# The queries of seven token blocks from seven half-size products instead of four full ones, with their cosine product put elsewhere and two rooms for the rotation

## The chip, the cores and the metric

The kernel runs on one core of a Trainium2 chip, as one launch. The metric is the device time of a whole execution in microseconds (us); the time of a kernel is the median of its runs. The profile is one more execution, taken by the hardware profiler. All data are float32.

The engines by the profile's names: PE is the matrix engine (PEld its loading of weights), DVE the vector engine, ACT the scalar engine, POOL GpSimd, and SP the queue that issues most DMAs. PE writes its products to PSUM, from which DVE and ACT read them.

## The reference, cut to what matters

A graph layer is followed by attention and a mixture of experts, over 4096 tokens of 256 features:

```python
def layer(x, adj, ...):
    f = layernorm(x)
    x = x + concat([f, (adj @ (f @ neigh_W.T)) / (adj.sum(1) + 1)]) @ lin_W.T   # graph
    h = rmsnorm(layernorm(x), ln1_w)
    q, k, v = h @ wq.T, h @ wk.T, h @ wv.T                     # 4 heads of q, 2 of k and v, 64 wide
    q = q * cos + rotate_half(q) * sin                         # the same for k
    ...                                                        # causal attention, projection
    ...                                                        # router, 2 of 8 experts, their sum
```

`rotate_half` puts the negated second half of a head before its first half. The change is in how `h @ wq.T` and the rotation of q are computed.

## The kernel before, in words

The tokens are eight blocks of 512. The first stage is the graph layer. `aggregate(b)` makes the product of adjacency row block b with the features, over eight steps jb. A step takes one 512 x 512 block of the adjacency, 1 MB, which `load` brings with a lead of three steps into three buffers `a`. Each step already uses Strassen's scheme in Winograd's form: `halve` makes the sums and differences S1 to S4 of the adjacency block on DVE (lines 495 to 498), one step ahead of their use; `halve_x` made those of the features earlier (lines 467 to 470); and PE does seven products of halves, in two parts each, into four PSUM tiles (line 538). S1 and S2 of even steps lie in the room of the last block's queries, and those of odd steps in `more_sums`. At the end of a row block DVE puts the seven products together (lines 547 to 560, line 546 on ACT).

Into the steps of `aggregate(b)` other work is sewn in at fixed places, between the fourth and the fifth of the seven products of a step or at its end: the last linear map of the row block before (`linear`, line 199), and from `qkv(b - 1)` the queries, keys and values of that row block. There is no scheduler: each engine takes its instructions in the order in which the program writes them. For a block, `qkv` does this:

- step 1: `scales` (statistics) and `turn_tables` (the tables of cosines and sines are transposed),
- step 2: `norm` and `leave` (the normed rows go to DRAM); at its end `fetch` brings them back into a room called `z`, and `spread_tables` copies the tables to all partitions,
- step 3, end: `turn` transposes `z` on DVE into `qT[b]`, features on partitions and tokens along the row (line 621),
- step 4: `values_and_logits` (line 632), then `turned_heads((2,))`, which makes k,
- step 5: `turned_heads((0, 1))`, which makes the two halves of q.

`turned_heads` multiplies on PE, 512 tokens wide, two products for each of its parts (line 648), into a PSUM tile of pool `p_pj`, which has two. DVE multiplies the result by the cosines (line 655), straight from PSUM into its place; four ACT copies put the swapped and signed quarters into the room `rot` (line 657); POOL multiplies them by the sines and adds them (lines 661 and 662). `rot` has one room, so the copies of the next part wait for POOL's addition. The room `z` is the place of the next block's queries, for the seventh block a tile of its own, `last_z`. The eighth block goes another way, in the attention stage.

The stages after it are attention with routing and then the experts. They are not touched.

Of the kernel before, what the change touches and what calls it, by code (L numbers as in the profile page):

```python
# [9 lines left out]
F32 = mybir.dt.float32  # L10
I32 = mybir.dt.int32
SP = mybir.EngineType.SP
AF = mybir.ActivationFunctionType
# [4 lines left out]
P = 128  # L18
# [4 lines left out]
NH, NKV, HD = 4, 2, 64  # L23
# [8 lines left out]
Q = HD // 2  # L32
# [34 lines left out]
def fast_kernel(  # L67
# [24 lines left out]
    nc = tc.nc  # L92
# [27 lines left out]
    for e in range(NE):  # L120
# [6 lines left out]
    wqkv_sb = const.tile([P, 2, 512 + NE], F32, name="wqkv_sb")  # L127
# [14 lines left out]
    qT = [  # L142
        qT_all[:, b * 1024 : (b + 1) * 1024].rearrange("p (c i) -> p c i", c=2)
        for b in range(NB)
    ]
# [43 lines left out]
    def in_order(x):  # L189
        return x.rearrange("p (g c d) -> p c g d", g=4, c=2)  # L190
# [68 lines left out]
    with (  # L259
# [37 lines left out]
        tables = {}  # L297
# [50 lines left out]
        def bounds():  # L348

            ps = p_pj.tile([P, 512], F32, tag="pj", name="p_bounds")  # L350
            gram = ps[:, 0 : 3 * HD].rearrange("p (m i) -> p m i", m=3)
            for m in range(3):
                for c in range(2):
                    for j in range(2):
                        head = wqkv_sb[:, c, m * P + j * HD : m * P + (j + 1) * HD]
                        nc.tensor.matmul(
                            gram[j * HD : (j + 1) * HD, m, :], head, head,
                            start=(c == 0), stop=(c == 1), skip_group_check=True,
                        )
            squares = gx.tile([P, HD], F32, tag="rot", name="squares", bufs=1)  # L360
            for m in range(3):
                nc.scalar.activation(
                    squares, gram[:, m, :], AF.Square, accum_out=norms[:, m : m + 1]
                )
# [12 lines left out]
        def router_wo():  # L377
            transposed_wo = qT[5][:, :, 0:C]
            ps = p_pj.tile([P, 512], F32, tag="pj", name="p_wo")
            for j in range(2):  # L380
                for c in range(2):
                    nc.tensor.matmul(
                        ps[:, j * NE : (j + 1) * NE], transposed_wo[:, c, j * P : (j + 1) * P],
                        wqkv_sb[:, c, QK : QK + NE], start=(c == 0), stop=(c == 1),
                    )
            nc.scalar.copy(
                wo_sb[:, :, C:], ps[:, 0 : 2 * NE].rearrange("p (j e) -> p j e", j=2)
            )

        def negate_weights():  # L390
            for k in range(2):
                nc.scalar.activation(
                    wn_less[:, k, :], wn_sb[:, k, :], AF.Identity,
                    bias=wn_sb[:, k, C - 1 : C], scale=-1.0,
                )
            nc.gpsimd.memset(m_sb[:, 0, C : C + 1], 0.0)
            nc.gpsimd.tensor_copy(m_sb[:, 1, C : C + 1], ident[:, P - 1 : P])
# [21 lines left out]
        G11, G12, G21, G22, T1, T2, T4 = range(7)  # L419
        T3 = G12  # L420
        HC = C // 2
        g = [gw.tile([P, 7, 2, HC], F32, name=f"g{b}") for b in range(NB)]
# [145 lines left out]
            )  # L568

        turning = [tc.dram_tile([512, C], F32, name=f"turning{n}") for n in range(2)]  # L570
        last_z = gs.tile([P, 1024], F32, name="last_z")

        def qkv(b):

            made = {}

            def scales():
                stats(gx, b)
                var = mv[b][:, :, 1:2]
                power(both[b], var, *BOTH)  # L580
                power(rstd[b], var, 1.0, EPS_LN)

            def norm():

                made["h0"] = [
                    t.rearrange("p (t c) -> p t c", t=2)
                    for t in (kT[b], vv[b].rearrange("p t c -> p (t c)"))
                ]
                for t in range(TB):
                    nc.vector.tensor_scalar(  # L590
                        in_order(made["h0"][t // 2][:, t % 2, :]), in_groups(res[b][:, t, :]),
                        mv[b][:, t, 0:1], both[b][:, t], op0=ALU.subtract, op1=ALU.mult,
                    )
                made["ratio"] = ratio(gx, b)

            def leave():

                for n, h0 in enumerate(made.pop("h0")):
                    nc.sync.dma_start(
                        turning[b % 2][n * 2 * P : (n + 1) * 2 * P].rearrange(  # L600
                            "(t p) c -> p t c", p=P
                        ),
                        h0,
                    )

            def fetch():

                made["z"] = qT_all[:, (b + 1) * 1024 : (b + 2) * 1024] if b + 2 < NB else last_z
                squares = turning[b % 2].rearrange("(m i) (g e) -> g i m e", i=Q, g=4)
                for n in range(4):  # L610
                    nc.sync.dma_start(
                        made["z"][n * Q : (n + 1) * Q].rearrange("p (m e) -> p m e", e=2 * Q),
                        squares[n],
                    )

            def turn():

                made["hT"] = qT[b]
                z = made.pop("z").rearrange("p (m c d) -> p c m d", c=2, d=Q)
                for c in range(2):  # L620
                    nc.vector.transpose(
                        qT[b][:, c, :].rearrange("p (m i) -> p m i", i=Q), z[:, c]
                    )

            def values_and_logits():
                for h in range(2):
                    pj = p_tr.tile([P, 2, 2, P], F32, tag="tr", name=f"pv_{b}_{h}")
                    pj = pj.rearrange("p c t i -> p c (t i)")
                    for i in range(2):
                        at = (2 * h + i) * P  # L630
                        for c in range(2):
                            nc.tensor.matmul(  # L632
                                pj[:, i, 0 : NE + P], made["hT"][:, c, at : at + P],
                                wqkv_sb[:, c, QK:], start=(c == 0), stop=(c == 1),
                            )
                    nc.scalar.copy(vv[b][:, 2 * h : 2 * h + 2, :], pj[:, :, NE : NE + P])  # L636
                    for i in range(2):
                        t = 2 * h + i
                        nc.scalar.activation(
                            first_lg[b][:, t, :], pj[:, i, 0:NE], AF.Copy,  # L640
                            scale=made["ratio"][:, t],
                        )

            def turned_heads(ms):
                pjs = [p_pj.tile([P, 512], F32, tag="pj", name=f"pq_{b}_{m}") for m in ms]
                for m, pj in zip(ms, pjs):
                    for c in range(2):
                        nc.tensor.matmul(
                            pj, wqkv_sb[:, c, m * P : (m + 1) * P], made["hT"][:, c, :],
                            start=(c == 0), stop=(c == 1),  # L650
                        )
                for m, pj in zip(ms, pjs):
                    to = kT[b] if m == 2 else qT[b][:, m, :]
                    rot = gx.tile([P, 512], F32, tag="rot", name=f"rot_{b}_{m}", bufs=1)
                    nc.vector.tensor_mul(to, pj, tables[b][:, 0, :])  # L655
                    for n in range(4):
                        nc.scalar.activation(  # L657
                            rot[n * Q : (n + 1) * Q, :], pj[(n ^ 1) * Q : ((n ^ 1) + 1) * Q, :],
                            AF.Copy, scale=1.0 if n % 2 else -1.0,
                        )  # L660
                    nc.gpsimd.tensor_mul(rot, rot, tables[b][:, 1, :])  # L661
                    nc.gpsimd.tensor_add(to, to, rot)

            return [
                [scales, lambda: turn_tables(b)], [norm, leave], [],
                [values_and_logits, lambda: turned_heads((2,))], [lambda: turned_heads((0, 1))],
            ], {
                (2, "end"): [fetch], (2, "loaded"): [lambda: spread_tables(b)],
                (3, "end"): [turn],
            }  # L670
# [34 lines left out]
                steps[jb, "end"] = [lambda b=jb + 3: turned_x(b)]  # L705
        steps[0].insert(1, lambda: turned_x(2))
        steps[3].append(load_rest)
        for jb, f in ((5, scale_rest), (6, bounds), (6, turn_wo), (7, router_wo)):
            steps[jb].append(f)
        behind, at_end = [], []  # L710
        for b in range(NB):
# [15 lines left out]
    with (  # L727
# [76 lines left out]
        probs, sums, accs, ys, flats, chosen, squares, picks, narrows = ({} for _ in range(9))  # L804
# [2021 lines left out]
```

## Time and profile before

| what | value |
|---|---|
| median of 3 runs | 1512.95 us (1511.27 to 1515.51) |
| the profiled execution's own time | 1511.47 us |
| its span, first to last instruction | 1509.8 us |
| PE busy | 1496.9 us, 99% |
| DVE busy | 1083.9 us, 72% |
| ACT busy, POOL busy | 544.9 us, 568.9 us |
| line 648, products of q and k | 84 records of 592 ns |
| line 655, DVE product with the cosines | 21 of 0.69 us |
| line 657, ACT copies into `rot` | 84 of 589 ns |
| line 661, POOL product with the sines | 21, 1636 ns in the mean |

A float32 matmul leaves two records, each with its load of weights. The duration of a record includes the flow through the array, in which the next one already runs, so durations add up to more than the time that PE needs; the distance between two starts is what a record costs. A row "x8" of the timeline is eight records in a run.

### The profile page before, as it was taken

The page shows a single profiled execution, that of the slowest core. Times are in us where ns is not written, and L with a number is a line of the kernel's source. Part 1 is how long each engine was busy: PE and PEld are TensorE (multiplying, and loading weights), DVE is VectorE, ACT ScalarE, POOL GpSimd, SP SyncE. Part 2 cuts the span into 40 slices and gives each one's busy share as a digit, 9 for nine tenths or more (in the row PEclk, how much of TensorE's full clock was granted, in tenths as well). Part 3 has the DMA queues.
Part 4 walks back from the last instruction along what each step waited for, and adds up shares of the span by engine and source line. Part 5 has one row for each costly group of instructions (what it writes and reads, how often), then busy time and mean ns, then how long its engine had stood idle before and what let it go on. Part 6 is the DMA issues. An engine that isn't in the chain of part 4 may idle for free. (4 is left out here: it accounts for less than half of the span.)

```text
span 1509.8 us, 28585 instructions
## 1 busy us (share of the span) xinstructions
PE 1496.9 (99%) x10731; PEld 1102.8 (73%) x10731; DVE 1083.9 (72%) x2239; ACT 544.9 (36%) x975; POOL 568.9 (38%) x649
## 2 busy tenths in 40 slices
PE   9999999999999999999999999999999999999997
PEld 7888888888888544444444444358899999999996
DVE  7855666656765577779879879795676877777872
ACT  2102011021020455655665655653222334343341
POOL 2102122121221331374565553551523464554542
PEclk9999999999999999999999999999999999999999
DMA  7435645555566000011010110029977898999965
GB/s 244 133 119 178 201 147 173 166 170 171 162 184 185 21 15 22 24 59 30 30 59 28 36 41 30 30 87 336 251 180 225 254 278 233 264 272 246 270 155 135
DMA packets 127005, 220.56 MB, mean 146 GB/s; under 512 B 79530, under 2 KB 103338, under 8 KB 113226
## 3 DMA queue, kind: packets, MB, share of 16 engines
q1 hardware_dynamic: 113322, 200.39, 42.3%
q0 software_dynamic: 12720, 17.47, 6.6%
q8 instruction: 86, 1.41, 0.4%
q10 hardware_dynamic: 816, 0.79, 0.2%
q14 instruction: 61, 0.50, 0.1%
HBM read 188.67 MB, written 31.33 MB: 146 GB/s over the span
## 5 line engine op out<-in xcount | busy, mean ns | idle before, releaser
L826 PE MATMUL sc<-qT_all,kT 64*64 64x512 f32 (+3 forms) x2304 | 282.1, 557 | 0.5 <-ACT pt_all L834 0.3
L538 PE MATMUL acc<-a,g 128*128 128x256 f32 x1024 | 244.0, 379 | 0.0
L538 PEld LDWEIGHTS acc<-a,g 128*128 128x128 f32 x1024 | 194.1, 190 | 32.2 <-issue 6.7
L826 PEld LDWEIGHTS sc<-qT_all,kT 64*64 64x64 f32 x2304 | 91.3, 133 | 128.9 <-issue 109.9
L834 ACT ACTIVATE pt_all<-sc 128x1024 f32<-128x1024 f32 (+3 forms) x157 | 149.0, 956 | 99.9 <-PE sc L826 95.6
L1917 POOL DMA_INDIRECT acc_dram<-y,late x40 | 63.3, 1583 | 177.0 <-ACT y L1906 118.9
L538 PE MATMUL acc<-more_sums,g 128*128 128x256 f32 x512 | 126.3, 379 | 0.0
L854 DVE TENSOR_TENSOR late<-late,pt_all 128x1024 f32<-128x1024 f32 (+3 forms) x92 | 106.6, 1159 | 20.4 <-ACT pt_all L834 9.0
L661 POOL TENSOR_TENSOR rot<-rot,tables 128x512 f32<-128x512 f32 x21 | 34.4, 1636 | 192.4 <-ACT rot L657 137.3
L538 PEld LDWEIGHTS acc<-more_sums,g 128*128 128x128 f32 x512 | 97.2, 190 | 13.2
L868 PE MATMUL y_second<-pt_all,vv 64*64 64x512 f32 (+3 forms) x440 | 105.0, 555 | 0.0
L868 PE MATMUL y_first<-pt_all,vv 64*64 64x512 f32 (+3 forms) x440 | 104.3, 553 | 0.0
L1837 PE MATMUL h<-late,qT_all 128*128 128x256 f32 (+1 forms) x616 | 104.0, 327 | 0.0
L1837 PEld LDWEIGHTS h<-late,qT_all 128*128 128x128 f32 x616 | 93.5, 191 | 9.6 <-ACT late L1521 0.8
L1110 POOL DMA_INDIRECT lists<-row,slots x64 | 91.3, 1426 | 17.2 <-issue 14.5
L636 ACT COPY vv<-pv 128x256 f32<-128x256 f32 x14 | 5.2, 373 | 251.9 <-PE pv L632 216.0
L868 PE MATMUL y_third<-pt_all,vv 64*64 64x512 f32 (+3 forms) x376 | 89.8, 557 | 0.0
L1844 DVE TENSOR_TENSOR late<-si,h 128x256 f32<-128x256 f32 (+2 forms) x87 | 39.3, 466 | 64.4 <-ACT si L1843 44.6
L657 ACT ACTIVATE rot<-pq 32x512 f32<-32x512 f32 x84 | 49.5, 589 | 82.5 <-DVE qT_all L655 33.1
L1843 ACT ACTIVATE si<-h 128x256 f32<-128x256 f32 (+2 forms) x87 | 36.1, 418 | 107.0 <-PE h L1837 93.1
L538 PE MATMUL acc<-qT_all,g 128*128 128x256 f32 x256 | 65.7, 379 | 0.0
L854 DVE TENSOR_TENSOR sum_all<-sum_all,pt_all 128x1024 f32<-128x1024 f32 (+3 forms) x49 | 53.5, 1093 | 15.8 <-POOL pt_all L836 9.9
(480 smaller groups left out, 3321.4 us busy)
## 6 DMA issues: line engine op xcount, KB each, us to landing
a<-in_adj_dram SPq DMA_DIRECT2D x64, 1024.0 KB
qT_all<-in_w_dram SPq DMA_DIRECT2D x18, 1408.0 KB
pt_all<-in_w_dram SPq DMA_DIRECT2D x16, 1408.0 KB
res_all<-in_w_dram SPq DMA_DIRECT2D x17, 768.0 KB
pt_all<-in_w_dram SPq DMA_DIRECT2D x16, 768.0 KB
res_all<-in_w_dram SPq DMA_DIRECT2D x8, 1408.0 KB
qT_all<-in_w_dram SPq DMA_DIRECT2D x9, 768.0 KB
late<-lists SPq DMA_DIRECT2D x96, 64.0 KB
```

What stands on the lines that cost most here:

```text
L538: nc.tensor.matmul(acc[bank][:, at, :], g[jb][:, right, k, :], m[left][:, k, :], start=(jb == 0 and k == 0 and at == 0), stop=(jb == NB - ...
L657: nc.scalar.activation(rot[n * Q : (n + 1) * Q, :], pj[(n ^ 1) * Q : ((n ^ 1) + 1) * Q, :], AF.Copy, scale=1.0 if n % 2 else -1.0,)
L661: nc.gpsimd.tensor_mul(rot, rot, tables[b][:, 1, :])
L826: nc.tensor.matmul(ps[k * HP : (k + 1) * HP, j, :w], kT[sb][hd, i * P + k * HP : i * P + (k + 1) * HP], qT[b][hd, p, off:], start=True, st ...
L834: nc.scalar.activation(pt[:, :, :w], ps[:, :, :w], AF.Exp, scale=HD ** -0.5)
L854: nc.vector.tensor_add(sums[b, p][:, :, off:], before[:, :, off:], pt[:, :, : 512 - off])
L868: nc.tensor.matmul(accs[b, p][k][hd, off:], vv[sb][some, i, hd], pt[some, j, : 512 - off], start=(s == order_of(b)[0]), stop=(s == order_o ...
L1110: put = nc.gpsimd.indirect_dma_start(out=lists[:, :], out_offset=bass.IndirectOffsetOnAxis(ap=chosen[b][:, k, t, :], axis=0), in_=flats[b] ...
L1837: nc.tensor.matmul(ps[m % 2][:, m // 2 - q, :], w13_sb[:, c, m * P : (m + 1) * P], xT[:, c, :], start=(c == 0), stop=(c == 1),)
L1843: nc.scalar.activation(si[:, 0:both, :], ps[0][:, 0:both, :], AF.Silu)
L1844: nc.vector.tensor_mul(hT[:, q : q + both, :], si[:, 0:both, :], ps[1][:, 0:both, :])
L1917: put = nc.gpsimd.indirect_dma_start(out=(acc_dram if k < NM - LAST else out)[:, :], out_offset=at, in_=y[:, h, :], in_offset=None, comput ...
```

## The change

Instead of two times two products of 128 x 128 weights with 512 tokens, the query weights (256 x 256) and the tokens `hT` (256 x 512) are each cut into four quarters, and q is made by Strassen's seven products of a 128 x 128 quarter of weights with 256 tokens (`seven_heads`, at step 5).

- The sums of the weights, `sums_q`, are made once on POOL (`sum_heads`, in step 7 of the first row block).
- The sums of the tokens, T1 to T4, are made on DVE at the beginning of step 4 (`sums_h`), into the room `z`, which is kept for that.
- The seven products lie two by two in four PSUM tiles: two of `p_pj` and two of `p_tr`. One ACT copy and seven DVE additions put them together in `qT[b]`.
- The rotation then reads `qT[b]` in SBUF rather than PSUM. The product with the cosines goes to `z`, and POOL adds it to the rotated part into `qT[b]`.
- `rot` has two rooms. `last_z` is now a part of the features of the first block, `g[0]`, which are no longer needed then.
- Keys, values and the eighth block are as before, but k's part also uses the two rooms.

```diff
-            squares = gx.tile([P, HD], F32, tag="rot", name="squares", bufs=1)
+            squares = gx.tile([P, HD], F32, tag="rot", name="squares", bufs=2)
...
+        sums_q = gw.tile([P, 4, P], F32, name="sums_q")
...
+        def sum_heads():
+            m = heads_q
+            nc.gpsimd.tensor_add(m["S1"], m["A21"], m["A22"])
+            nc.gpsimd.tensor_sub(m["S2"], m["S1"], m["A11"])
+            nc.gpsimd.tensor_sub(m["S3"], m["A11"], m["A21"])
+            nc.gpsimd.tensor_sub(m["S4"], m["A12"], m["S2"])
...
-        last_z = gs.tile([P, 1024], F32, name="last_z")
+        last_z = g[0].rearrange("p n k i -> p (n k i)")[:, 0:1024]
...
+            def sums_h():
+                m = made["m"] = {
+                    f"B{c + 1}{h + 1}": qT[b][:, c, h * 2 * P : (h + 1) * 2 * P]
+                    for c in range(2) for h in range(2)
+                }
+                room = made["z"].rearrange("p (n i) -> p n i", n=4)
+                m.update((f"T{n + 1}", room[:, n]) for n in range(4))
+                nc.vector.tensor_sub(m["T1"], m["B12"], m["B11"])
+                nc.vector.tensor_sub(m["T2"], m["B22"], m["T1"])
+                nc.vector.tensor_sub(m["T3"], m["B22"], m["B12"])
+                nc.vector.tensor_sub(m["T4"], m["T2"], m["B21"])
+
+            def seven_heads():
+                m = {**heads_q, **made.pop("m")}
+                banks = [
+                    p_pj.tile([P, 2, 2 * P], F32, tag="pj", name=f"pq_{b}_{n}") for n in range(2)
+                ] + [
+                    p_tr.tile([P, 2, 2, P], F32, tag="tr", name=f"pq_{b}_{n}").rearrange(
+                        "p c t i -> p c (t i)"
+                    ) for n in range(2, 4)
+                ]
+                p = {}
+                for n, (number, left, right) in enumerate((
+                    (1, "A11", "B11"), (2, "A12", "B21"), (6, "S2", "T2"), (7, "S3", "T3"),
+                    (5, "S1", "T1"), (3, "S4", "B22"), (4, "A22", "T4"),
+                )):
+                    p[number] = banks[n // 2][:, n % 2, :]
+                    nc.tensor.matmul(
+                        p[number], m[left], m[right], start=(n % 2 == 0), stop=True,
+                        skip_group_check=True,
+                    )
+                u2 = u4 = m["B12"]
+                u3 = m["B22"]
+                nc.scalar.copy(u2, p[1])
+                nc.vector.tensor_add(m["B11"], u2, p[2])
+                nc.vector.tensor_add(u2, u2, p[6])
+                nc.vector.tensor_add(u3, u2, p[7])
+                nc.vector.tensor_add(u4, u2, p[5])
+                nc.vector.tensor_add(m["B12"], u4, p[3])
+                nc.vector.tensor_sub(m["B21"], u3, p[4])
+                nc.vector.tensor_add(m["B22"], u3, p[5])
+                products = made.pop("z").rearrange("p (k i) -> p k i", k=2)
+                for k in range(2):
+                    to = qT[b][:, k, :]
+                    rot = gx.tile([P, 512], F32, tag="rot", name=f"rot_{b}_{k}", bufs=2)
+                    for n in range(4):
+                        nc.scalar.activation(
+                            rot[n * Q : (n + 1) * Q, :], to[(n ^ 1) * Q : ((n ^ 1) + 1) * Q, :],
+                            AF.Copy, scale=1.0 if n % 2 else -1.0,
+                        )
+                    nc.vector.tensor_mul(products[:, k], to, tables[b][:, 0, :])
+                    nc.gpsimd.tensor_mul(rot, rot, tables[b][:, 1, :])
+                    nc.gpsimd.tensor_add(to, products[:, k], rot)
...
-                    rot = gx.tile([P, 512], F32, tag="rot", name=f"rot_{b}_{m}", bufs=1)
+                    rot = gx.tile([P, 512], F32, tag="rot", name=f"rot_{b}_{m}", bufs=2)
...
-                [values_and_logits, lambda: turned_heads((2,))], [lambda: turned_heads((0, 1))],
+                [sums_h, values_and_logits, lambda: turned_heads((2,))], [seven_heads],
...
-        for jb, f in ((5, scale_rest), (6, bounds), (6, turn_wo), (7, router_wo)):
+        for jb, f in ((5, scale_rest), (6, bounds), (6, turn_wo), (7, router_wo), (7, sum_heads)):
```

More of the change, by code (lines that the diff above doesn't have):

```diff
@@ L388, in router_wo @@
             )
+        sums_q = gw.tile([P, 4, P], F32, name="sums_q")
+        heads_q = {
+            f"A{r + 1}{c + 1}": wqkv_sb[:, c, r * P : (r + 1) * P]
+            for r in range(2) for c in range(2)
+        }
+        heads_q.update((f"S{n + 1}", sums_q[:, n]) for n in range(4))
+        def sum_heads():
[4 more added lines that the diff above has]
+            nc.gpsimd.tensor_sub(m["S4"], m["A12"], m["S2"])
         def negate_weights():
@@ L618, in turn @@
                 made["hT"] = qT[b]
-                z = made.pop("z").rearrange("p (m c d) -> p c m d", c=2, d=Q)
+                z = made["z"].rearrange("p (m c d) -> p c m d", c=2, d=Q)
                 for c in range(2):
@@ L642, in values_and_logits @@
                         )
+            def sums_h():
+                m = made["m"] = {
+                    f"B{c + 1}{h + 1}": qT[b][:, c, h * 2 * P : (h + 1) * 2 * P]
+                    for c in range(2) for h in range(2)
+                }
+                room = made["z"].rearrange("p (n i) -> p n i", n=4)
[4 more added lines that the diff above has]
+                nc.vector.tensor_sub(m["T4"], m["T2"], m["B21"])
```

## The prediction

> **What bounds the kernel now.** I read the page first, then the busy time by row block (windows of 58.8 us, one period of `aggregate`), then the timeline around the products that are replaced.
>
> ```profile
> span 1509.8 us, 28585 instructions
> PE 1496.9 (99%) x10731; PEld 1102.8 (73%) x10731; DVE 1083.9 (72%) x2239; ACT 544.9 (36%) x975; POOL 568.9 (38%) x649
> ...
> PEclk9999999999999999999999999999999999999999
> ```
>
> PE is busy from end to end at full clock. In the stage of the change:
>
> ```profile
> 132.80:191.60 58.80, 58.80 (x270) 49.70 (x269) 39.77 (x75) 10.01 (x21) 13.25 (x10) 1.00 0.55 172
> 426.80:485.60 58.80, 58.80 (x270) 49.70 (x269) 39.00 (x71) 8.84 (x19) 12.62 (x10) 1.00 0.55 171
> ```
>
> PE 58.80 of 58.80; then PEld 49.7, DVE 39 to 40, ACT 9 to 10, POOL 13. Busy PE is modelled, so I looked at starts: between 100 and 505 us they follow each other without a hole. So only two things count here: PE time removed, and any wait that PE newly meets.
>
> ```profile
> 370.20 1.89 PE L538 MATMUL acc<-more_sums,g 128*128 128x256 f32 x8
> 371.93 3.60 PE L648 MATMUL pq<-qT_all,wqkv_sb 128*128 128x512 f32 x8
> 375.36 0.81 PE L538 MATMUL acc<-a,g 128*128 128x256 f32 x3
> ```
>
> Eight 256-wide records take 371.93 - 370.20 = 1.73 us, 0.216 us each; eight 512-wide ones take 375.36 - 371.93 = 3.43 us, 0.429 each. The reader is to see that half the width costs half the time.
>
> **PE: what goes.** Per block 8 records x 0.429 = 3.43 us go, and 7 products x 2 records x 0.216 = 3.02 us come: 0.41 us less, in seven blocks **-2.9 us**. [...] I take -2.9. More weight loads (190 ns each) lie under 0.216 us of streaming, as in line 538.
>
> **DVE, step 4.** Four subtractions 128x256, SBUF from SBUF, go before k's product with the cosines and before the halving for step 6 (line 495 and on). The nearest rows are line 467 with 0.42 us and the like:
>
> ```profile
> L467 DVE TENSOR_TENSOR g<-g x8: 418/420/423, 14.7 to 79.7; 128x256 f32<-128x256 f32 x8
> ```
>
> Lines 467 to 470 start 0.45, 0.35 and 0.45 us apart, so four are 1.6 us. They stand in the queue behind the halving for step 5, which waits for its adjacency block. In the first block:
>
> ```profile
> 130.90 0.69 DVE L495 TENSOR_TENSOR more_sums<-a 128x512 f32<-128x512 f32 x1 [4.16 <-DMA a<-in_adj_dram]
> ...
> 133.63 0.68 DVE L655 TENSOR_TENSOR kT<-pq,tables 128x512 f32<-128x512 f32 x1
> ```
> ```profile
> 134.41 2.40 ACT L657 ACTIVATE rot<-pq 32x512 f32<-32x512 f32 x4 [4.63 <-DVE kT L655]
> ```
> ```profile
> 136.63 3.60 PE L648 MATMUL pq<-qT_all,wqkv_sb 128*128 128x512 f32 x8
> ```
>
> k's PSUM tile is free when these ACT copies end. The second tile of q takes its place. Before, PE comes to that tile after four wide records, 1.72 us after q's start; now after two narrow products, 0.86 us after. In the seven blocks the copies now end 0.17, -2.65, -0.25, -1.55, -1.45, -1.33 and -1.01 us from q's start. With 1.6 us added: 1.77, -1.05, 1.35, 0.05, 0.15, 0.27 and 0.59. Past 0.86 are the first (0.91) and the third (0.49): with a hand-over of about 0.1 us each, **PE waits 1.6 us in all**. This wait is new. T2 and T3 are ready before it: in the first block the subtractions end at about -1.3.
>
> **DVE, steps 5 to 7.** After the products come seven additions with a PSUM operand, by lines 547 to 560 (0.42 us, 0.35 to 0.46 apart) 3.0 us, and two multiplications of 0.69; before only those two. The third addition overwrites B22, which the sixth product reads, so it starts 2.8 us after q's start (2.58 and the 0.2 that a hand-over from PE takes, as in line 655's start at 374.70 behind its last reader), and the chain goes on from there. The halving for step 7 then begins some 5.9 us after q's start, not 4.24: 1.7 later. Now the collisions:
>
> ```profile
> 378.02 0.69 DVE L497 TENSOR_TENSOR more_sums<-a,more_sums 128x512 f32<-128x512 f32 x1
> 378.05 1.79 POOL L661 TENSOR_TENSOR rot<-rot,tables 128x512 f32<-128x512 f32 x1 [4.47 <-DVE more_sums L496]
> 378.62 1.76 DVE L498 TENSOR_TENSOR a<-a 128x512 f32<-128x512 f32 x1
> ```
>
> Beside POOL a DVE operation of 0.68 us takes 1.76, and POOL's 1.27 becomes 1.79: they take turns. [...] The change turns two multiplications from a PSUM to an SBUF input, adds four subtractions of that kind, and, with two rooms, sends POOL's four operations one after the other, about 7 us without a pause, instead of two and two. By the row, one collision costs DVE 1.07 us; four behind q are 4.3. Taken in turns, the halving for step 7 ends at about 12.5 us after q's start. PE wants S3, its last sum, as fourth product of step 7: 3.02 + six products of 0.43 + a step of 6.03 + three of 0.86 = 14.2. Margin 1.7. The next halving, which today waits for its DMA until about 11.1, ends near 16.5, and line 547, which frees the first accumulator, at 17.0; PE comes back to that at 17.7. Margin 0.7. So I cost these at nothing, hidden by 14 and more us of matmuls of steps 5 to 7. [...]
>
> **ACT and POOL.** One copy of 0.37 us a block comes (line 636's row), and ACT is idle for most of the time. POOL has the same four operations for q; the two rooms take ACT's wait for POOL away (25.5 us in all in the waits) and end POOL's work about 2 us sooner, but PE waits for none of this, so it brings 0. In the seventh block POOL ends at about 503 us, before 504.3; attention's first exp is at 508.98. `sum_heads` is four 128x128 operations behind the weights' scaling (ended at 75.2 us), at 0.3 to 0.5 us by line 661's 1.27 for four times the width: 2 us on an idle POOL, which could delay DVE by as much; 0 to 1 us, I take 0, as their first use is 60 us later. No DMA is added or moved. `last_z` in `g[0]` is written at step 2's end, past that buffer's last use in step 0.
>
> **Sum.** 1509.8 - 2.9 + 1.6 = 1508.5 us span, with the 1.7 us around it (1511.47 - 1509.8) 1510.2. The profiled run lay 1.5 us under the median; on the median 1512.95 - 1.3 = **1511.7**.
>
> **The rivals.**
> - *Full gain.* DVE's four subtractions fall where it was waiting, the adjacency block comes a little sooner, and PE meets no wait: 1512.95 - 2.9 = 1510. For it: five of seven blocks show none. Against it: blocks one and three lack the room.
> - *DVE becomes late (slower).* Place: S3 of step 7 and the first accumulator. If the additions take turns with k's POOL work, the chain is 2 us later, past the margin 0.7 by 1.3, in each of six blocks 1.3 us (8 us) with 1.6 for the PSUM tile, less 2.9: +6.7, 1519.7. It decides from 0.9 us of lateness per block on (0.7 margin plus about 0.2), where it eats the remaining 1.3. Against it: no lengthened PSUM row.
> - *k's tile is late everywhere (slower, smaller).* With adjacency blocks 1 us later, the tile waits are 1.9, 0, 1.5, 0.2, 0.3, 0.4 and 0.7: 5.0 us, +2.1, 1515. At 2 us later they are 11, +8.
> - *It does not do what it says.* If matmuls with fresh weights were bound by their loads, 14 x 0.19 = 2.7 us is still less than 3.02, so this costs nothing.
>
> **How the numbers follow.** Main case 0.45; full gain 0.25; k's tile late 0.17; DVE late 0.13. 0.3% is 4.5 us, about what a measurement of this kernel can tell from no change (its three runs spread by 4.2). The PE saving cannot reach that; only a run-to-run shift could: 0.06 faster. Slower by over 4.5 are most of DVE late and the far end of the tile's wait: 0.14. The rest, 0.80, is the same. The range goes from the full gain with 1.5 us of measurement, 1508.5, to past the tile case and into the DVE case, 1518.
>
> **What would show it.** Right: q's line with 98 records 256 wide, 0.216 us apart; 3.02 us a block where it meets no wait; a hole in PE of 0.5 to 1 us ahead of the third product in the first and third block; no hole at the end of step 7; span about 1508.5. Wrong: holes in every block ahead of the third product; PE waiting for line 498's or 547's successor at step 7 or at the next block's start; PSUM additions of over 1 us; records of 256 further than 0.23 us apart.

## The result and the profile after

| | median us | runs | range |
|---|---|---|---|
| kernel before, in this comparison | 1511.57 | 20 | 1511.09 to 1515.51 |
| changed kernel | 1509.64 | 20 | 1507.88 to 1511.39 |

The ratio is 0.9986, with a 95% interval of 0.998 to 0.9992: 1.9 us less by the medians, where 1.3 was forecast. That is within 0.3%, and yet clear of no change. The profiled execution took 1510.23 us.

The page of the changed kernel:

```profile
span 1508.5 us, 28795 instructions
...
PE 1495.7 (99%) x10773; PEld 1111.8 (74%) x10773; DVE 1116.2 (74%) x2316; ACT 550.2 (36%) x982; POOL 566.6 (38%) x653
```

PE gives up 1.2 us of busy time and is still busy from end to end; DVE has 32 us more to do and nobody sees it in the span. The windows by row block (columns: window, its length, the busy time of PE, PEld, DVE, ACT and POOL, granted clock, DMA share, GB/s):

```profile
132.80:191.60 58.80, 58.80 (x277) 51.19 (x277) 41.15 (x79) 9.63 (x20) 12.66 (x10) 1.00 0.55 170
191.60:250.40 58.80, 58.45 (x275) 50.58 (x274) 42.47 (x83) 9.62 (x20) 12.56 (x10) 1.00 0.54 171
...
426.80:485.60 58.80, 58.80 (x277) 50.90 (x276) 43.32 (x85) 9.63 (x20) 11.93 (x10) 1.00 0.55 170
```

One thing is new: in the second window PE is no longer busy all the time, 58.45 of 58.80. The timeline shows where. First PE, then ACT, then DVE in front of it, all of the changed kernel:

```profile
195.13 1.03 PE L687 MATMUL pq<-qT_all,wqkv_sb 128*128 128x256 f32 x4
196.50 1.99 PE L687 MATMUL pq<-qT_all,sums_q 128*128 128x256 f32 x8 [0.35 <-ACT rot L727]
198.34 0.59 PE L687 MATMUL pq<-qT_all,wqkv_sb 128*128 128x256 f32 x2
198.77 1.03 PE L552 MATMUL acc<-a,g 128*128 128x256 f32 x4
```
```profile
194.06 2.39 ACT L727 ACTIVATE rot<-pq 32x512 f32<-32x512 f32 x4 [5.79 <-DVE kT L725]
```
```profile
189.06 0.69 DVE L509 TENSOR_TENSOR more_sums<-a 128x512 f32<-128x512 f32 x1 [5.08 <-DMA a<-in_adj_dram]
...
191.20 0.68 DVE L512 TENSOR_TENSOR a<-a 128x512 f32<-128x512 f32 x1
191.80 0.42 DVE L666 TENSOR_TENSOR qT_all<-qT_all 128x256 f32<-128x256 f32 x1
...
192.93 0.42 DVE L669 TENSOR_TENSOR qT_all<-qT_all 128x256 f32<-128x256 f32 x1
193.26 0.69 DVE L725 TENSOR_TENSOR kT<-pq,tables 128x512 f32<-128x512 f32 x1
```

The halving for step 5 (lines 509 to 512) waits 5.08 us for its adjacency block. The four sums (666 to 669) stand behind it and ahead of k's product with the cosines (725); its four copies end at 196.45; the third of the seven products, the first into k's old PSUM tile, starts at 196.50. The first two products end their share at 195.99, so PE stands for 0.5 us, and the next record comes 0.1 us late too: a wait of 0.6 us (the window shows less of it, as the ends of busy records are modelled). Two more of 0.1 and 0.24 us are in the third and sixth blocks.

From here on I use the *stage*: the time from the first record of the aggregation (line 538, or 552 after) to the first one of the scores in attention (line 826, or 896), and *holes*: by how much the starts of PE's records lie further apart there, from 100 us on, than 0.216 us for 256 columns and 0.429 for 512. Before, the stage is 489.1 us with no hole; after, 487.2 with 0.95. 2.88 saved less 0.95 is 1.93, which is the change of the stage. That the medians differ by the same 1.9 is in part chance. In the four sets of comparisons the median of the kernel before was 1511.6, 1512.8, 1512.8 and 1513.1 us, and the time behind the stage varies by 1.4 us between the profiled executions (1001.3 to 1002.6). In the later sets the distance to the kernel before comes out larger than any stage explains: the split kernel below has a stage 0.17 us longer than that of the kernel before, and a median 1.24 us shorter. Where the kernel before took the time, no trace of those executions shows. So the stage is the measure here, and medians are compared within one set.

### The profile page after: what moved, and what is told of

Read it like the earlier page. It is cut to its first block, busy times and chain, and to the rows that moved or that the text cites. A ratio compares the mean times of both kernels' runs of the same rounds, so it can differ in the third digit from the quotient of the medians.

```text
span 1508.5 us, 28795 instructions
## 1 busy us (share of the span) xinstructions
PE 1495.7 (99%) x10773; PEld 1111.8 (74%) x10773; DVE 1116.2 (74%) x2316; ACT 550.2 (36%) x982; POOL 566.6 (38%) x653
## 4 chain that ended last, share of the span: by engine, by line
PE 94%; DMA 2%; POOL 1%; DVE 1%; issue 1%; ACT 1%; SPq 0%; POOLq 0%; DVEq 0%; ACTq 0%
PE acc L552 25%; PE sc L896 14%; PE h L1907 13%; PE y_second L938 5%; PE y_third L938 5%; PE ye_y L1961 4%; PE y_first L938 4%; PE hA L1724 4%; PE ye_y L1864 3%; PE ye_ms L1864 3%; PE hD L1724 2%; PE pf L523 2%; PE ph L199 2%; PE pq L687 1%; PE po L1018 1%; PE hB L1724 1%
## 5 line engine op out<-in xcount | busy, mean ns | idle before, releaser
L731 POOL TENSOR_TENSOR rot<-rot,tables 128x512 f32<-128x512 f32 x7 | 9.0, 1279 | 156.1 <-ACT rot L727 156.1
L904 ACT ACTIVATE late<-sc 128x1024 f32<-128x1024 f32 (+3 forms) x55 | 50.8, 927 | 39.0 <-PE sc L896 31.4
```

Of the source, the lines that this page charges most:

```text
L904: nc.scalar.activation(pt[:, :, :w], ps[:, :, :w], AF.Exp, scale=HD ** -0.5)
```

## The experiments

**The changed kernel again.**

> The changed kernel once more, as the measure for its companions on one chip. My theory (PE-bound stage; 2.9 us of matmuls saved, less a wait of PE for k's PSUM tile ahead of the third of the seven products in the blocks whose adjacency data land late): 1.6 to 2.4 us under the kernel before, with 0.5 to 1.6 us of holes at the third product, in different blocks from execution to execution. Rival (DVE is what takes the rest of the gain, at step 7 or the next block's first accumulator): holes there instead.

1509.74 us against 1512.81, ratio 0.998 (0.9972 to 0.9988). The 3.1 us are more than was expected, and more than the 2.88 that the products save; the surplus is the unexplained one above. Stage 487.9, holes 1.69 us: 0.13, 1.15, 0.10 and 0.30 in the first, third, fourth and sixth blocks, all at the third product or just behind it. So the wait is there in both executions, in other blocks. They follow the arrival of the adjacency block for step 5: in the three profiled executions with this order of work (these two, and the run with one room below) PE waited in exactly the 11 of 21 blocks in which the halving for step 5 began at most 6.6 us before q's start. In the others it began at least 6.79 before. In 10 of the 11 the halving had waited for that DMA.

**Other PSUM tiles.** It tells apart whether PE waits for k's tile or for DVE.

```diff
                 banks = [
-                    p_pj.tile([P, 2, 2 * P], F32, tag="pj", name=f"pq_{b}_{n}") for n in range(2)
-                ] + [
                     p_tr.tile([P, 2, 2, P], F32, tag="tr", name=f"pq_{b}_{n}").rearrange(
                         "p c t i -> p c (t i)"
-                    ) for n in range(2, 4)
+                    ) if n in (1, 2) else
+                    p_pj.tile([P, 2, 2 * P], F32, tag="pj", name=f"pq_{b}_{n}")
+                    for n in range(4)
                 ]
```

> The four PSUM tiles of the seven products in the order pj, tr, tr, pj, so that k's tile is taken by the seventh product instead of the third: 1.7 us more time for k's copies. My theory: the holes at the third product go and none comes elsewhere; 0.5 to 1.6 us under the changed kernel, 2.9 under the kernel before. Rival (DVE): the same time as the changed kernel within 0.3 us.

1509.19 us, 0.9974 (0.9965 to 0.9983). The holes at the products are gone, as expected; but the stage is 487.3 with one new hole of 1.10 us in another place, in the sixth block. It has nothing to do with the tiles directly (waits of this kernel between 410 and 425 us):

```profile
DVE qT_all L635 <- DMA qT_all<-turning: 7.2, 1, 7.2
...
PE pv L646 <- DVE qT_all L635: 0.6, 1, 0.6
```

The normed rows came back from DRAM 2 us later than in the other blocks, so `turn` and then the values were late. "None elsewhere" was wrong. It is the way out to DRAM that was slow: the queue waited for the write of the rows and issued their reading 4.24 us after its second part, against 2.33 to 2.35 in the second to fifth blocks. The three kernels with these tiles all have this hole in the same block; the kernel with the split products below has the same slow write (4.02 us) without a hole, so the tiles are not needed for it. Why the write is slow there wasn't settled.

**The sums behind k.**

```diff
-                [sums_h, values_and_logits, lambda: turned_heads((2,))], [seven_heads],
+                [values_and_logits, lambda: turned_heads((2,)), sums_h], [seven_heads],
```

> The four token sums on DVE are moved behind k's product with the cosines, so that k's copies start 1.6 us earlier. My theory: the holes at the third product go unless T2 itself is late (it is ready about 0.9 us before q's start in the latest block of the profile before); 0.5 to 1.6 us under the changed kernel. If the wait were for T2 rather than for the tile: no better, or worse by up to 0.5 us.

1508.32 us, 0.9971 (0.9962 to 0.9981), and no hole at all: stage 486.3, 2.84 us under the kernel before, for 2.88 worked out. The same windows, of this kernel:

```profile
132.80:191.60 58.80, 58.80 (x277) 51.22 (x276) 45.40 (x86) 10.68 (x22) 13.13 (x10) 1.00 0.54 170
191.60:250.40 58.80, 58.80 (x277) 51.20 (x276) 42.55 (x78) 8.55 (x19) 13.01 (x10) 1.00 0.55 170
426.80:485.60 58.80, 58.80 (x277) 51.12 (x276) 45.03 (x85) 10.56 (x22) 12.39 (x10) 1.00 0.56 171
```

PE is busy throughout again. T2 was not late. Together with the run before it, this shows the wait to be for the tile, and what it costs: against the changed kernel in the same set the median is 1.4 us less.

**One room for the rotation.**

```diff
-                    rot = gx.tile([P, 512], F32, tag="rot", name=f"rot_{b}_{k}", bufs=2)
+                    rot = gx.tile([P, 512], F32, tag="rot", name=f"rot_{b}_{k}", bufs=1)
...
```

The same edit is made at the two other places that use this room.

> The rotation has one room again, all else as in the changed kernel. My theory: PE waits for none of the rotation, so the time stays within 0.5 us of the changed kernel, although POOL's work for q ends about 2 us later in a block and ACT waits for POOL again (20 us and more in the waits). Rival (the two rooms brought a part of the gain): 1 us or more slower than the changed kernel.

1509.89 us, 0.9975 (0.9968 to 0.9982): as the changed kernel. In its waits ACT stands behind POOL again, as before the change, and this costs nothing:

```profile
ACT rot L706 <- POOL qT_all L712: 24.9, 7, 3.6
```

Its stage, 488.8, has more holes in the profiled execution (2.60), but again only at the third product, where the second room plays no part; by the times of the runs there is no difference.

**The sums twice over**, alone and with the other order of tiles.

```diff
                 nc.vector.tensor_sub(m["T4"], m["T2"], m["B21"])
+                nc.vector.tensor_sub(m["T1"], m["B12"], m["B11"])
+                nc.vector.tensor_sub(m["T2"], m["B22"], m["T1"])
+                nc.vector.tensor_sub(m["T3"], m["B22"], m["B12"])
+                nc.vector.tensor_sub(m["T4"], m["T2"], m["B21"])
```

> The four token sums are made twice over (same values), so that k's copies and the release of k's PSUM tile come another 1.6 us later. My theory: PE's wait at the third product grows in every block that has it and starts in most others; with the copies' ends of the profile before plus 3.2 us against 0.86 us: 2.5, 0, 2.1, 0.8, 0.9, 1.0 and 1.3 us, about 8.6 in all; 6 to 8 us slower than the changed kernel, 1515 to 1518 us. Rival (the tile is not what PE waits for, or DVE's lateness counts at step 7): no growth at the third product; within 1 us of the changed kernel, or holes at step 7.

> The sums twice over as in the run before, and the PSUM tiles in the order pj, tr, tr, pj, so that k's tile is wanted at 2.58 us instead of 0.86. My theory: most of that loss goes, holes of 0 to 1.5 us are left, 1508.5 to 1511 us. Rival (extra DVE work is dear by itself): as slow as with the sums twice over alone.

Alone: 1518.71 us, 1.0041 (1.0025 to 1.0056), stage 496.1 with 9.8 us of holes; a little dearer than expected. With the other tiles: 1509.69, 0.9978 (0.997 to 0.9986), stage 488.1 with 1.8 us, of which 1.0 is the late return of the sixth block and 0.8 is a wait at the last product, where k's tile is now wanted. So the same extra DVE work costs 9 us or next to nothing, by which tile the third product takes. About 1.7 of the 9.8 us are no wait. After the longest one, 2.35 us, PE's records are 0.43 us apart instead of 0.216, at a granted clock of 0.50. Windows of the run with the sums twice over: the wait, what follows it, and what follows a shorter wait of 1.7 us (the last column but two is the granted clock):

```profile
196.30:198.60 2.30, 0.11 (x2) 0.03 (x1) 2.16 (x4) 2.24 (x5) 0.00 (x0) 1.00 0.01 4
199.75:203.15 3.40, 3.40 (x9) 2.66 (x8) 2.18 (x6) 0.42 (x1) 1.38 (x2) 0.50 0.00 0
319.70:323.10 3.40, 3.40 (x16) 3.01 (x17) 2.31 (x7) 0.31 (x1) 2.53 (x2) 1.00 0.01 5
```

**More DVE work behind the products.** Four more multiplications, to find the margin that hides what the change added.

```diff
+                    nc.vector.tensor_mul(products[:, k], to, tables[b][:, 0, :])
+                    nc.vector.tensor_mul(products[:, k], to, tables[b][:, 0, :])
                     nc.vector.tensor_mul(products[:, k], to, tables[b][:, 0, :])
```

> Each product with the cosines of q is made three times (same values), so that DVE has 4 more operations of 0.69 us behind the seven products, ahead of the halving for step 7. It sizes the margin that hides the changed kernel's extra DVE work. In its profile the first accumulator is free 1.7 to 1.8 us before PE comes back to it at the next row block. My theory: with 2.4 to 2.8 us more PE waits there 0.7 to 1 us in six blocks; 4 to 7 us slower than the changed kernel, 1513.5 to 1516.5. Rival (DVE's lateness is taken up elsewhere, in its waits for adjacency data): within 1 us of the changed kernel. If my margin of 0.7 from the prediction were right: about 2 us in each of six blocks, 11 to 13 us slower.

1519.9 us, 1.0047 (1.0031 to 1.0062), stage 498.2 with 12 us of holes: 10 us over the changed kernel, more than I expected, and not where I expected it. PE waits in step 7 for S2 (line 510) and S3 (512), 1.5 us in each of seven blocks, not for the accumulators. The waits of this kernel:

```profile
PEld acc L552 <- DVE more_sums L510: 7.2, 6, 1.2
PE acc L552 <- DVE more_sums L510: 4.8, 6, 0.8
PEld acc L552 <- DVE a L512: 3.6, 6, 0.6
```

The timeline shows why 2.8 us of work became 6.8 us of lateness for S2:

```profile
203.72 0.69 DVE L712 TENSOR_TENSOR qT_all<-qT_all,tables 128x512 f32<-128x512 f32 x1
204.31 1.27 POOL L713 TENSOR_TENSOR rot<-rot,tables 128x512 f32<-128x512 f32 x1 [4.70 <-ACT rot L706]
204.33 1.79 DVE L710 TENSOR_TENSOR qT_all<-qT_all,tables 128x512 f32<-128x512 f32 x1
...
206.16 1.64 DVE L711 TENSOR_TENSOR qT_all<-qT_all,tables 128x512 f32<-128x512 f32 x1
...
210.18 1.57 DVE L510 TENSOR_TENSOR more_sums<-more_sums,a 128x512 f32<-128x512 f32 x1
```

POOL's first operation starts 1.96 us after the last PSUM addition here and 1.95 in the changed kernel, however much DVE has to do behind it. The four delay whichever four DVE operations they meet, by about 1 us each (1.79, 1.64, 1.64 and 1.57 us here, where these take 0.69 alone). In the changed kernel the first one comes just after S2 has started (202.60 and 202.56 us), and two of the four hits fall on the next halving, which has time. With more work ahead, all four fall on or ahead of S2: 2.8 us of work and four times 1 us.

**The products cut, without the sums.** The kernel before with q's four products in eight halves. By the rows of the kernel before two narrow records take 2 x 0.216 = 0.432 us and a wide one 0.429, so 2 to 3 ns would be a record's own; this run measures it.

```diff
+                    for i in range(1 if m == 2 else 2):
+                        at = slice(0, 512) if m == 2 else slice(i * 2 * P, (i + 1) * 2 * P)
...
-                            pj, wqkv_sb[:, c, m * P : (m + 1) * P], made["hT"][:, c, :],
+                                pj[:, at], wqkv_sb[:, c, m * P : (m + 1) * P],
+                                made["hT"][:, c, at], start=(c == 0 and i == 0), stop=(c == 1),
```

> The kernel before, with each of q's four products cut into two of 256 tokens: eight products, no sums, no other change. It measures the fixed cost of a narrower matmul by itself. My theory (2 to 3 ns for a record): records 0.216 us apart, 3.45 instead of 3.43 us a block; the time of the kernel before within 0.3 us. [...]

1511.54 us, 0.9991 (0.9983 to 0.9999): the median is 1.24 us under the kernel before, where none was expected. The stage is 489.3, 0.17 us over it, so the work of the stage does not make the median shorter. Its timeline:

```profile
371.95 3.62 PE L650 MATMUL pq<-qT_all,wqkv_sb 128*128 128x256 f32 x16
375.40 0.81 PE L538 MATMUL acc<-a,g 128*128 128x256 f32 x3
```

Sixteen records in 375.40 - 371.95 = 3.45 us are 0.216 us each. Here the narrower product has no price of its own beyond 2 to 3 ns.

**Both cures, and the sums behind k once more.**

> Both cures of the tile wait together: token sums behind k's product, and the PSUM tiles in the order pj, tr, tr, pj. My theory: no wait is left for k's tile, so this reaches the floor of the seven products, 2.9 us under the kernel before in the stage, and no more than the sums behind k alone, within 0.7 us of it. If a wait of PE for that tile were still hidden in executions other than the profiled one: up to 0.7 us better.

> The sums behind k alone once more, beside the run with both, on one chip: 1508 to 1509.5 us, 3 to 4.5 us under the median of the kernel before as it stood in the first set.

Both: 1509.57 us, 0.9978 (0.9972 to 0.9985), stage 487.3. The floor was missed, and the run is 1.3 us slower than the one with the sums behind k alone: there is no wait at the products, but the late return of the sixth block is there again (1.06 us). The sums behind k alone: 1508.27, 0.9971 (0.996 to 0.9981), stage 486.2, no hole. Its median was under that of the changed kernel both times, by about 1.4 us (the second time across sets), and it is the best version found: the change, with one list entry moved. The intervals of the two ratios overlap, so the difference is firmer in the holes than in the ratio.

**The sums three times over**, for the clock.

> The four token sums made three times over. With them twice, one wait of PE of 2.35 us was followed by 3.4 us at half the granted clock, and waits of 1.71 us by none. If the length of the wait decides: here several waits lie between 2.3 and 4 us, and each of those is followed by some 3.4 us at half clock, 1.7 us dearer than the wait itself; 1524 to 1534 us. If that one dip was chance: none or one dip, and 11 us over the run with twice, as the waits add up.

1531.19 us in one run. The time lies in the first forecast's range, but neither account held: there were seven waits of 1.3 to 3.2 us and three dips of the clock, after waits of 2.18, 2.99 and 3.15 us, but not after 2.87, 2.85 and 2.59. So the length of the wait alone did not decide it; windows of this run are in the last section.

## Why the prediction was right, point by point

- *PE saves 2.9 us.* Shown: 2.84 in the stage of the kernel with no hole. The price of a narrow product that the rows gave, 2 to 3 ns a record, held: the split kernel has 28 more products (56 more records) and a stage 0.17 us longer, which is 3 ns for each of these records.
- *PE waits for k's tile, 1.6 us in all.* The mechanism is shown by the other tiles, the other order and the sums twice over. The size was 0.95, 1.69 and 2.60 us in three profiled executions that are alike in this, so 1.6 is about the middle of a wide range. The step that missed is the list of blocks: I took the copies' ends of one profile as fixed, and named the first and third; after, the holes were in the second, third and sixth. They vary with the DMA of the adjacency, so only the sum could be forecast.
- *DVE's and POOL's work is hidden.* Right, with more margin than I worked out. In the first block the halving for step 7 began 6.0 us after q's start (5.9 forecast) but ended at 10.9, not 12.5, and line 561 freed the first accumulator at 15.9, not 17.0: the collisions begin later than I had put them, and two of the four fall on the next halving. The margins at S3 and at the accumulator were then 3.3 and 1.8 us, not 1.7 and 0.7. Four more multiplications did turn it over, at S2, which the margins had left out, rather than at the accumulators. The rival "DVE becomes late" is real, but the change does not reach it.
- *The two rooms bring nothing.* Shown by the run with one room.
- *PSUM additions collide with POOL: 0.* Right, and tested: in the changed kernel 20 of the 49 additions (lines 694 to 700) run beside k's POOL work, 12 of them from end to end, and all take 0.41 to 0.42 us, as lines 547 to 560 do in every record of the kernel before (406 to 422 ns). The 2 us a block of the rival "DVE becomes late" were an estimate, two collisions of 1.07 us; no run shows one at a PSUM addition. From the first block of the changed kernel:

```profile
137.99 1.27 POOL L732 TENSOR_TENSOR kT<-kT,rot 128x512 f32<-128x512 f32 x1
```
```profile
138.19 0.42 DVE L694 TENSOR_TENSOR qT_all<-qT_all,pq 128x256 f32<-128x256 f32 x1 [1.40 <-ACT qT_all L693]
138.72 0.42 DVE L695 TENSOR_TENSOR qT_all<-qT_all,pq 128x256 f32<-128x256 f32 x1
```

The forecast of the median, 1511.7, stood on a median of 1512.95 from three runs; over twenty it was 1511.57, and 1.3 less would have been 1510.3 against 1509.64. That the forecast of the span, 1508.5, was met to the tenth is in part luck. The stage became 1.93 us shorter rather than 1.3, as the waits came to 0.95 in that execution and not 1.6; the time ahead of it and behind it, where the change saves nothing, was 0.7 us longer.

## What to carry to other kernels

On a stage where PE has no hole, the price of a change is the distance between starts of its records, plus the waits that it makes; busy sums of the other engines say little. When a product is cut into smaller ones, each PSUM tile is wanted earlier (here k's 0.86 us after q's start instead of 1.72), so give the tile that comes free last to the product that is issued last, or put new DVE work behind the work that frees it. Work that another engine hides has its margin at the first thing that PE wants from the queue, and collisions with POOL, about 1 us each here, fell on whatever stood there at the time.

## What the runs showed of the hardware

Some of PE's waits were followed by half the granted clock. In the run with the sums twice over, the wait of 2.35 us was followed by a window of 3.40 us (199.75 to 203.15) with a granted clock of 0.50, in which the records came 0.43 us apart instead of 0.216: 1.7 us on top of the wait. Behind its wait of 1.7 us the window from 319.70 to 323.10 had 1.00. With the sums three times over, three of seven waits were followed by a dip: those of 2.18, 2.99 and 3.15 us, and not those of 2.87, 2.85 and 2.59. Windows behind four of the waits of that run:

```profile
140.95:144.35 3.40, 3.40 (x10) 2.68 (x9) 2.27 (x7) 0.63 (x1) 1.35 (x2) 0.50 0.02 5
202.40:205.80 3.40, 2.92 (x7) 2.39 (x8) 1.48 (x4) 0.80 (x2) 2.53 (x2) 0.50 0.03 5
267.25:270.65 3.40, 3.40 (x18) 2.99 (x17) 2.85 (x8) 1.46 (x3) 1.08 (x1) 1.00 0.00 0
448.15:451.55 3.40, 2.99 (x7) 2.45 (x8) 1.42 (x3) 0.73 (x2) 2.53 (x2) 0.50 0.00 0
```

PE leaves 18 records in the window at 1.00 and 7 to 10 in those at 0.50. What decides about a dip, besides the length of the wait, was not shown.

The clock also fell after the last product of an execution, and not at the same distance. In the kernel before PE's last record starts at 1500.58; the granted clock was 1.00 up to 1506.15 and 0.50 from 1506.20 on:

```profile
1499.35:1502.75 3.40, 1.61 (x8) 1.08 (x6) 0.48 (x1) 0.00 (x0) 1.86 (x3) 1.00 0.06 11
1502.80:1506.15 3.35, 0.00 (x0) 0.00 (x0) 0.00 (x0) 0.00 (x0) 1.32 (x1) 1.00 0.72 83
1506.20:1509.70 3.50, 0.00 (x0) 0.00 (x0) 0.00 (x0) 0.00 (x0) 0.00 (x0) 0.50 0.01 2
```

In the changed kernel the last record starts at 1499.43, and the clock was 0.50 from 1502.40 on:

```profile
1498.90:1502.30 3.40, 0.91 (x5) 0.45 (x3) 0.48 (x1) 0.00 (x0) 3.01 (x3) 1.00 0.33 42
1502.40:1508.00 5.60, 0.00 (x0) 0.00 (x0) 0.00 (x0) 0.00 (x0) 0.12 (x1) 0.50 0.24 28
```

So half clock began 5.6 us after the start of the last record in the one and 2.9 us in the other, with no record of PE behind it in either.
